# A token list made by one-hot products and gathered expert tiles in place of scattered ones, in a deformable convolution with a mixture-of-experts FFN

## The chip, the cores and the metric

One core of a Trainium2 chip runs the whole program. The metric is the device time of one execution, in microseconds; the kernel before has a median of 8195.0 us over nine runs (8178.31 to 8216.84). Everything is in float32.

## The reference

The input x is 4 images of 256 channels, 64 by 64. The layer computes

```python
x = x + conv3(ln_c(x))            # three deformable 3x3 convolutions, each with relu
t = to_tokens(x)                  # 4 images of 4096 tokens of 256 values
t = t + ffn(ln_t(t))
```

A deformable convolution computes 27 offset channels with an ordinary 3x3 convolution: a shift (dy, dx) and a mask for each of the 9 taps and each pixel. For each tap it samples the input bilinearly at the shifted place, multiplies by the mask, and multiplies the 256 sampled channels by that tap's 256x256 weights; the nine products are summed.

The FFN has 8 experts. A softmax over 8 gate logits picks the two likeliest experts of a token, and

```python
for e in range(8):
    h = gelu(xf @ w1[e] + b1[e])          # 256 -> 512
    out += cw[:, e:e+1] * (h @ w2[e] + b2[e])   # 512 -> 256
```

where cw is the softmax value at the two chosen experts and 0 elsewhere. So each token needs only two of the eight, and the kernel computes only these.

## The kernel before

**Convolution.** There are 12 stages, one for each image and layer. A stage has 8 blocks of 512 pixels, and a block 9 taps, so the program has 864 taps in all (`main_block`, L437 to L505). For each tap, POOL issues four indirect DMAs g (L452), each of which fetches for 128 pixels a row of 4 KB from a table in DRAM that holds two neighbouring pixels, values and differences. DVE interpolates in one direction (L458), ACT scales the first neighbour (L463), DVE adds the second (L468), PE transposes the samples (L472), ACT copies them out of PSUM (L477), and PE multiplies them with the tap's weights into `acc` (L480). The g buffers number ten, so POOL can run about two and a half taps ahead. The offset convolutions, the tables of the next layer and the gate of finished images are cut into pieces that `step` inserts after taps.

**The FFN, one group an image.** A group has M = 32 token tiles of 128 and NF = 39 expert tiles of FT = 256 slots (two chosen experts a token make 8192 slots, or 32 tiles, and each of the 8 experts may leave a tile partly filled). `tokens` writes t (the residual) and z (the normalised tokens) to DRAM and computes gate weights. When an image's last block is done, `enqueue` (L820) puts the group's steps in a queue, each with a price in taps:

- `route` (price 0) counts how many tokens go to each expert and gives each of a token's two choices a slot number; the slots of one expert begin at a multiple of 256. It also makes `wrow`, the rows of the weight table for every expert tile. Where a tile has the same expert as the tile two before, which used the same buffer, the rows are put out of bounds, and the fetch moves nothing.
- `dispatch_load` and `dispatch`: z is loaded again in blocks of 4 tiles (`zl`, L675, on SP), and each of the 64 pieces of 128 tokens is scattered by POOL to its slots in a DRAM array `zs` (L681). A dispatch step is one token tile with two scatters and costs 0.5 taps.
- 39 `expert` steps: POOL fetches the weights of the next tile (`w`, L706, 128 rows of 9.2 KB, two buffers), SP loads 256 slots of z (`zt`, L726), PE transposes them (`ftp`, L739), multiplies with W1 (`ph`, L750), ACT applies gelu (`hT`, L760), PE multiplies with W2 (`py`, L765), DVE adds the bias (`y`, L773), and SP stores y to `ys`.
- 16 `combine` steps: each of two token tiles; t is loaded in blocks of four tiles (`ta`, L783, on SP), POOL gathers each token's two results (`gy`, L794), DVE adds them with their weights (L802), PE transposes, and SP stores the output (L816).

`pump` (L837) runs after every tap and takes steps from the queue as the credit of one per tap allows. Groups 0 and 1 are spread over 2.9 stages each (the expert tiles 4.25 taps apart), group 2 over 1.9 (2.40 taps apart). Group 3 belongs to the last stage; its steps run after all convolution, with nothing beside them, and are called the tail here.

Each engine runs its instructions in one order, which a scheduler fixes when the program is built from the order of the calls and its own estimates; an instruction that waits holds up all behind it on its engine or queue. On POOL these are g, the scatters, w and gy, all indirect DMAs. Every buffer's reuse is a wait: the second w buffer is free when `y` of the tile that used it has read its bias.

`ffn_constants` writes zeros to the two `zs` arrays at the start (38 DMAs of 512 KB and 2 of 256 KB on SP), so that empty slots hold finite numbers.

Of the kernel before, what the change touches and what calls it, by code (L numbers as in the profile page):

```python
# [8 lines left out]
F32 = mybir.dt.float32  # L9
I32 = mybir.dt.int32  # L10
AF = mybir.ActivationFunctionType
ALU = mybir.AluOpType
AX = mybir.AxisListType
WAIT, ORDER = (
    mybir.DependencyInfo(c, mybir.DependencyReason.DATA)
    for c in (mybir.DependencyClass.Sync, mybir.DependencyClass.NoSync)
)

P = 128
H = W = 64  # L20
C = 256
CC = C // P
K = 9
NL = 3
TPB = 4
BLK = P * TPB
NB = H * W // BLK
# [8 lines left out]
E = 8  # L36
# [3 lines left out]
FT = 1 << FT_LOG  # L40
FU = FT // P
# [31 lines left out]
class Group:  # L73


    def __init__(self, b, n0, n1):
        self.b, self.n0, self.n1 = b, n0, n1
        self.nm = f"{b}_{n0}"
        self.M = (n1 - n0) * TPB

        self.NF = 2 * self.M * P // FT + E - 1
        self.scatters = []


class Weave:
# [83 lines left out]
    def ffn_constants(self):  # L169
        nc, cst, ins = self.nc, self.cst, self.ins  # L170
        self.t_dram, self.z_dram = (
            [
                [
                    self.dram.tile([P, TPB, C], F32, name=f"{v}_{b}_{n}", tag=f"{v}_{b}_{n}")
                    for n in range(NB)
                ]
                for b in range(self.B)
            ]
            for v in ("t", "z")
        )  # L180
        nf = max(g.NF for g in self.groups)
        self.zs, self.ys = (
            [
                self.dram.tile([nf * FT, C], F32, name=f"{v}_{i}", tag=f"{v}_{i}")
                for i in range(2)
            ]
            for v in ("zs", "ys")
        )

        nil = self.big.tile([P, 4 * C], F32, tag="a", name="nil")  # L190
        nc.vector.memset(nil, 0.0)
        for z in self.zs:
            r = 0
            while r < nf * FT:
                k = min(4 * P, nf * FT - r)
                nc.sync.dma_start(
                    z[r : r + k, :].rearrange("(p q) c -> p (q c)", p=P), nil[:, : k // P * C]
                )
                r += k
        self.gw = cst.tile([P, CC, E], F32, name="gw")  # L200
# [26 lines left out]
        nc.vector.tensor_copy(self.part, part_i)  # L227
        tile_i = cst.tile([P, nf], I32, name="tile_i")
        nc.gpsimd.iota(tile_i, pattern=[[1, nf]], base=0, channel_multiplier=0)
        self.tile_f = cst.tile([P, nf], F32, name="tile_f")  # L230
        nc.vector.tensor_copy(self.tile_f, tile_i)

# [278 lines left out]
    def tokens(self, b, n, r):  # L511
# [4 lines left out]
        if n == grp.n0:  # L516
            grp.cw = self.rt2.tile([P, 2, grp.M], F32, tag="cw", name=f"cw_{grp.nm}")
            grp.sel = self.rt.tile([P, 2, E, grp.M], F32, tag="sel", name=f"sel_{grp.nm}")
            grp.slots = self.rt2.tile([P, 2, grp.M], I32, tag="slots", name=f"slots_{grp.nm}")
            grp.wrow = self.rt2.tile([P, grp.NF], I32, tag="wrow", name=f"wrow_{grp.nm}")  # L520
        xc = self.big.tile([P, CC, BLK], F32, tag="a", name=f"xr_{nm}")
# [17 lines left out]
        normalise(nc, self.small, tok, z, self.eps_t, nm)  # L539
        nc.sync.dma_start(self.z_dram[b][n], z)  # L540
        for t0 in range(0, TPB, 2):
# [68 lines left out]
    def route(self, grp):  # L610
# [36 lines left out]
        for i in range(2):  # L647
# [8 lines left out]
            past,  # L656
            self.tile_f[:, :NF].unsqueeze(2).to_broadcast([P, NF, E]),
            end.unsqueeze(1).to_broadcast([P, NF, E]),
# [8 lines left out]
        same = small("same", (P, NF))  # L667
        nc.vector.memset(same[:, 0:2], 0.0)
        nc.vector.tensor_tensor(same[:, 2:], ex[:, 2:], ex[:, : NF - 2], ALU.is_equal)
        nc.vector.scalar_tensor_tensor(rows, same, float(E * P), rows, ALU.mult, ALU.add)  # L670
        nc.vector.tensor_copy(grp.wrow, rows)

    def dispatch_load(self, grp, n):
        z = self.ffn.tile([P, TPB, C], F32, tag="c", name=f"zl_{grp.nm}_{n}")
        self.nc.sync.dma_start(z, self.z_dram[grp.b][grp.n0 + n])  # L675
        grp.z = z

    def dispatch(self, grp, n, t):
        m = n * TPB + t
        for i in range(2):  # L680
            ins = self.nc.gpsimd.indirect_dma_start(  # L681
                out=self.zs[grp.i % 2],
                out_offset=bass.IndirectOffsetOnAxis(ap=grp.slots[:, i, m : m + 1], axis=0),
                in_=grp.z[:, t, :],
                in_offset=None,
            ).ins


            if len(grp.scatters) > 1:
                self.tc.add_manual_dep(ins, grp.scatters[0].name, ORDER)  # L690
            if grp.scatters:
                self.tc.declare_no_dep(
                    ins, group=f"zs_{grp.nm}", keep=grp.scatters[:1] if len(grp.scatters) == 1 else (), reason="slots differ"
                )
            self.tc.add_to_no_dep_group(f"zs_{grp.nm}", ins)
            grp.scatters.append(ins)

    def weights(self, grp, f):
        if self.w is None:
            self.w = [  # L700
                self.wt.tile([P, 2, WINN], F32, tag="wt", name=f"w_{i}").rearrange(
                    "p a b -> p (a b)"
                )
                for i in range(2)
            ]
        self.nc.gpsimd.indirect_dma_start(  # L706
            out=self.w[f % 2][:, : W1N + W2N],
            out_offset=None,
            in_=self.ins["W"],
            in_offset=bass.IndirectOffsetOnAxis(ap=grp.wrow[:, f : f + 1], axis=0),  # L710
            bounds_check=E * P - 1,
            oob_is_err=False,
        )

    def expert(self, grp, f):

        nc = self.nc
        nm = f"{grp.nm}_{f}"
        if f == 0:
            self.weights(grp, 0)  # L720
        if f + 1 < grp.NF:
            self.weights(grp, f + 1)
        w = self.w[f % 2]
        w1, w2 = w[:, :W1N], w[:, W1N : W1N + W2N]
        zt = self.ffn.tile([P, FU, C], F32, tag="zt", name=f"zt_{nm}")
        load = nc.sync.dma_start(  # L726
            zt,
            self.zs[grp.i % 2][f * FT : (f + 1) * FT, :].rearrange("(p u) c -> p u c", u=FU),
        ).ins
        if f == 0:  # L730
            for s in grp.scatters[:-1]:
                self.tc.add_manual_dep(load, s.name, WAIT)
            grp.load = load
        else:
            self.tc.add_manual_dep(load, grp.load.name, ORDER)
        tp = self.ps.tile([P, CC, FT], F32, tag="tp", name=f"ftp_{nm}")
        for u in range(FU):
            for c in range(CC):
                nc.tensor.transpose(  # L739
                    tp[:, c, u * P : (u + 1) * P], zt[:, u, c * P : (c + 1) * P], self.ident  # L740
                )
# [21 lines left out]
        for u in range(FU):  # L763
# [12 lines left out]
        nc.sync.dma_start(  # L776
            self.ys[grp.i % 2][f * FT : (f + 1) * FT, :].rearrange("(p u) c -> p u c", u=FU),
            y,
        )

    def combine_load(self, grp, n):
        a = self.ffn.tile([P, TPB, C], F32, tag="c", name=f"ta_{grp.nm}_{n}")
        self.nc.sync.dma_start(a, self.t_dram[grp.b][grp.n0 + n])  # L783
        grp.acc = a

    def combine(self, grp, n, t0):
        nc = self.nc
        nm = f"{grp.nm}_{n}_{t0}"
        acc = grp.acc
        for t in range(t0, t0 + 2):  # L790
            m = n * TPB + t
            for i in range(2):
# [13 lines left out]
        for t in range(2):  # L806
            for c in range(CC):
                nc.tensor.transpose(
                    tp[:, c, t * P : (t + 1) * P],
                    acc[:, t0 + t, c * P : (c + 1) * P],  # L810
                    self.ident,
                )
# [7 lines left out]
    def enqueue(self, grp):  # L820

        nb = grp.n1 - grp.n0
        q = [(0, lambda: self.route(grp))]
        for n in range(nb):
            q.append((3 if n == 0 else 0, lambda n=n: self.dispatch_load(grp, n)))
            for t in range(TPB):
                q.append((0.5, lambda n=n, t=t: self.dispatch(grp, n, t)))
        taps = grp.stages * NB * K - (3 + 2 * nb + 4 + 4 + 2 * nb)
        for f in range(grp.NF):
            q.append((taps / grp.NF if f else 4, lambda f=f: self.expert(grp, f)))  # L830
        for n in range(nb):
            q.append((0 if n else 4, lambda n=n: self.combine_load(grp, n)))
            for t0 in range(0, TPB, 2):
                q.append((1, lambda n=n, t0=t0: self.combine(grp, n, t0)))
        self.queue += q
# [102 lines left out]
```

## Time and profile before

The profiled execution took 8198.5 us, 3.5 above the median; its span, from the first to the last instruction, is 8196.6 us.

| engine | busy us | share |
|---|---|---|
| PE (matmul) | 6740.6 | 82% |
| PEld (weight load, beside PE) | 3773.7 | 46% |
| DVE | 4918.2 | 60% |
| ACT | 3568.6 | 44% |
| POOL | 4506.9 | 55% |

| stage (us) | what runs beside the convolution |
|---|---|
| 2472 to 2663, 4412 to 4600, 6236 to 6442 | scatters of groups 0, 1, 2 |
| 2700 to 3700, 4700 to 5600 | experts of groups 0, 1 |
| 6478 to 7382 | experts of group 2 |
| 7390 to 7590 | combine of group 2, last blocks of convolution |
| 7666 to 8197 | tail: scatters, experts and combine of group 3, no convolution |

DMA moved 2314.45 MB, of which queue 0, that of all indirect DMAs, moved 1954.99 MB. The TensorE clock that was granted averages 0.922 of full speed.

A profile line such as `L681 POOL DMA_INDIRECT zs<-zl,slots x256 | 265.2, 1036 | 137.8 <-issue 71.9` reads: line 681, engine, operation, output and inputs, 256 of them; 265.2 us busy in all, 1036 ns each; the engine was idle 137.8 us just before them, and 71.9 us of it ended for no other reason than that the instruction was issued. A line of waits reads: who waited, for which instruction, how many us in all, how often, and the longest. An indirect DMA on POOL is busy while its descriptors are made; the data come later.

### The profile page before, as it was taken

How to read it: one execution, taken by the hardware profiler on the slowest of the kernel's cores; microseconds unless marked ns; L12 is line 12 of the kernel's file. 1: busy time of each engine (PE TensorE's matmuls, PEld its weight loads, DVE VectorE, ACT ScalarE, POOL GpSimd, SP SyncE). 2: the span in 40 equal slices, each digit the busy share in tenths (PEclk: the TensorE clock that was granted, in tenths of full speed). 3: DMA queues.
4: the chain of work that ended last, by engine and by line, in shares of the span. 5: the costliest groups of instructions: out<-in, count | busy, mean ns of one | idle time of the engine just before them, and what ended most of it. 6: DMA issues, size and time to landing. Idle time of an engine off the chain costs nothing. (4 is left out here: it accounts for less than half of the span.)

```text
span 8196.6 us, 91172 instructions
## 1 busy us (share of the span) xinstructions
PE 6740.6 (82%) x27032; PEld 3773.7 (46%) x27032; DVE 4918.2 (60%) x10768; ACT 3568.6 (44%) x7368; POOL 4506.9 (55%) x4133
## 2 busy tenths in 40 slices
PE   5898888888886999998867799999856889896395
PEld 2344334344442555555433455555532455563274
DVE  4776666667774666666665566667755555665201
ACT  3454444445542444545443444545433344443121
POOL 0564666566556566664566666665666554546413
PEclk8999999999998999999987999999978899998697
DMA  5987889889887898998787889998877777777433
GB/s 167 364 312 276 311 302 323 298 315 332 294 307 247 310 328 312 324 324 296 258 290 254 277 313 338 321 333 312 295 274 260 253 286 261 291 282 267 145 124 118
DMA packets 744472, 2314.45 MB, mean 282 GB/s; under 512 B 104345, under 2 KB 148377, under 8 KB 735785
## 3 DMA queue, kind: packets, MB, share of 16 engines
q0 software_dynamic: 544704, 1954.99, 67.5%
q1 hardware_dynamic: 199272, 353.64, 12.3%
q8 instruction: 216, 3.54, 0.2%
q14 instruction: 280, 2.29, 0.1%
HBM read 2167.35 MB, written 249.61 MB: 295 GB/s over the span
## 5 line engine op out<-in xcount | busy, mean ns | idle before, releaser
L452 POOL DMA_INDIRECT g<-tab,idx x3456 | 3800.6, 1100 | 2681.2 <-DVE s L468 1317.9
L480 PE MATMUL acc<-sT,wk 128*128 128x512 f32 x6912 | 3443.1, 643 | 383.0 <-ACT sT L477 249.7
L458 DVE SCALAR_TENSOR_TENSOR g<-g,cf 128x512 f32<-128x512 f32 x3456 | 2529.3, 745 | 451.8 <-DMA g<-tab,idx 358.1
L468 DVE SCALAR_TENSOR_TENSOR s<-g,cf,s 128x256 f32<-128x256 f32 x3456 | 1619.0, 482 | 1610.1 <-ACT s L463 1208.8
L463 ACT ACTIVATE s<-g,cf 128x256 f32<-128x256 f32 x3456 | 1674.1, 511 | 1669.4 <-DVE g L458 1127.7
L480 PEld LDWEIGHTS acc<-sT,wk 128*128 128x128 f32 x6912 | 1344.8, 204 | 2093.8 <-issue 1548.3
L472 PE MATMUL tp<-ident,s 128*128 128x128 f32 x6912 | 1085.4, 284 | 455.5 <-DVE s L468 313.1
L477 ACT COPY sT<-tp 128x512 f32<-128x512 f32 x1728 | 970.9, 587 | 1103.2 <-PE tp L472 685.2
L472 PEld LDWEIGHTS tp<-ident,s 128*128 128x128 f32 x6912 | 828.2, 145 | 939.7 <-issue 514.0
L765 PE MATMUL py<-w,hT 128*128 128x256 f32 x2496 | 636.1, 391 | 65.7 <-ACT hT L760 58.6
L750 PE MATMUL ph<-fzT,w 128*128 128x256 f32 x2496 | 619.2, 391 | 25.0 <-ACT fzT L743 11.9
L750 PEld LDWEIGHTS ph<-fzT,w 128*128 128x128 f32 x2496 | 479.7, 195 | 171.3 <-issue 49.1
L765 PEld LDWEIGHTS py<-w,hT 128*128 128x128 f32 x2496 | 458.2, 192 | 205.4 <-ACT hT L760 119.3
L706 POOL DMA_INDIRECT w<-in_W,wrow x156 | 178.3, 1143 | 647.8 <-issue 291.5
L760 ACT ACTIVATE hT<-ph,w 128x256 f32<-128x256 f32 x624 | 261.3, 470 | 522.6 <-PE ph L750 343.6
L328 PE MATMUL po<-win,wo 128*32 128x512 f32 x2304 | 451.8, 612 | 36.7 <-ACT win L263 24.8
L773 DVE TENSOR_TENSOR y<-py,w 128x512 f32<-128x512 f32 x156 | 107.6, 690 | 464.2 <-PE py L765 455.7
L794 POOL DMA_INDIRECT gy<-ys,slots x256 | 261.6, 1022 | 212.4 <-DVE ta L802 92.9
L681 POOL DMA_INDIRECT zs<-zl,slots x256 | 265.2, 1036 | 137.8 <-issue 71.9
L298 ACT COPY hv<-tpv 128x512 f32<-128x512 f32 x384 | 214.6, 595 | 194.6 <-PE tpv L293 133.7
L328 PE MATMUL po<-win_pre,wo 128*32 128x512 f32 x1152 | 231.8, 654 | 23.9 <-ACT win_pre L263 7.4
L739 PE MATMUL ftp<-ident,zt 128*128 128x128 f32 x624 | 99.6, 282 | 96.1 <-DMA zt<-zs 93.9
(144 smaller groups left out, 3305.1 us busy)
## 6 DMA issues: line engine op xcount, KB each, us to landing
tab<-hv SPq DMA_DIRECT2D x384, 256.0 KB
g<-tab,idx POOLq DMA_INDIRECT x3456
zt<-zs SPq DMA_DIRECT2D x156, 256.0 KB
ys<-y SPq DMA_DIRECT2D x156, 256.0 KB
wk<-in_conv_w SPq DMA_DIRECT2D x108, 256.0 KB
zs<-nil SPq DMA_DIRECT2D x38, 512.0 KB
xc_pre<-in_x SPq DMA_DIRECT2D x32, 512.0 KB
xr_tok<-in_x SPq DMA_DIRECT2D x32, 512.0 KB
```

Source lines behind the costliest of these rows:

```text
L328: nc.tensor.matmul(po[g * Q : (g + 1) * Q, :], lhsT=self.wo[l][:, k, c, :], rhs=w[:, c, ky : ky + RPB, kx : kx + W], start=(m < NQ), stop= ...
L452: nc.gpsimd.indirect_dma_start(out=g.rearrange("p x s f -> p (x s f)"), out_offset=None, in_=tb, in_offset=bass.IndirectOffsetOnAxis(ap=id ...
L458: nc.vector.scalar_tensor_tensor(g[:, :, 0, :], g[:, :, 1, :], cf[:, j, 0:1], g[:, :, 0, :], ALU.mult, ALU.add,)
L463: nc.scalar.activation(s, g[:, 0, 0, :], AF.Copy, scale=cf[:, j, 1:2])
L468: nc.vector.scalar_tensor_tensor(ss[u], gs[u][:, 1, 0, :], cf[:, j, 2:3], ss[u], ALU.mult, ALU.add)
L472: nc.tensor.transpose(tp[:, c, u * P : (u + 1) * P], ss[u][:, c * P : (c + 1) * P], self.ident,)
L477: nc.scalar.copy(sT[:, :, t0 * P : (t0 + 2) * P], tp)
L480: nc.tensor.matmul(acc[:, o, :], lhsT=self.wk[k][:, c, o * P : (o + 1) * P], rhs=sT[:, c, :], start=(k == 0 and c == 0), stop=(k == K - 1 ...
L681: ins = self.nc.gpsimd.indirect_dma_start(out=self.zs[grp.i % 2], out_offset=bass.IndirectOffsetOnAxis(ap=grp.slots[:, i, m : m + 1], axis=0),
L750: nc.tensor.matmul(ph[:, h, :], lhsT=w1[:, o : o + P], rhs=zT[:, c, :], start=(c == 0), stop=(c == CC - 1),)
L765: nc.tensor.matmul(py[:, u, :], lhsT=hT[h // 2][:, h % 2, u * P : (u + 1) * P], rhs=w2[:, h * C : (h + 1) * C], start=(h == 0), stop=(h == ...
L794: nc.gpsimd.indirect_dma_start(out=g, out_offset=None, in_=self.ys[grp.i % 2], in_offset=bass.IndirectOffsetOnAxis(ap=grp.slots[:, i, m : ...
```

## The change

The scatter of tokens to slots is replaced by its inverse. After `route`, every group makes a list `tok` that holds for each slot the number of the token in it, and the expert tiles gather their tokens by it.

- z is stored row by row in one DRAM array per group (`zd`). The arrays `zs`, their zero fill, the loads `zl` and the scatters are gone.
- `route` splits each slot number into slot & 127 and slot >> 7. An `invert` step, one token tile at a price of 0.25 taps, does the following twice (once for each choice): DVE compares a row of 0 to 127 with the low digit (`at`, 128x128), compares a row of 0 to 77 with the high digit and multiplies with the token number (`num`, 128x78), and PE adds at-transposed times num into a PSUM tile `inv` (128x78). After the 32nd step the sums are copied to `tok`, integers: column j of row p is the token in slot 128 j + p. Empty slots hold 0, so token 0 is computed there and never read.
- `fetch` issues on POOL, one step ahead of an expert tile, the weights w and two gathers zt of 128 rows of 1 KB by columns of `tok`, in two buffers for each half.
- The tiles are taken in the order 0, 20, 1, 21, 2, ...: even steps walk through the first half of the list and odd steps through the second, and each half has its own weight buffer. A fetch moves nothing when the tile before it in the list has the same expert.
- y is stored with the two halves of a tile one after the other in `ys`, which fits the order of `tok`.
- t is loaded for each pair of token tiles (256 KB in place of 512), and the load of the next pair is put ahead of the combine step of this one.
- Prices: inversion takes 8 taps in place of the dispatch's 16 and the rest is shared by the expert tiles, 4.46 taps apart in groups 0 and 1 and 2.61 in group 2.

```diff
+        self.half = (self.NF + 1) // 2
+        self.zt, self.acc = {}, []
+        self.order = [s // 2 + s % 2 * self.half for s in range(self.NF)]
...
-        for z in self.zs:
-            r = 0
-            while r < nf * FT:
-                k = min(4 * P, nf * FT - r)
-                nc.sync.dma_start(
-                    z[r : r + k, :].rearrange("(p q) c -> p (q c)", p=P), nil[:, : k // P * C]
-                )
-                r += k
+        for g in self.groups:
+            g.zd = self.dram.tile([g.M * P, C], F32, name=f"z_{g.nm}", tag=f"z_{g.nm}")
...
-        nc.vector.memset(same[:, 0:2], 0.0)
-        nc.vector.tensor_tensor(same[:, 2:], ex[:, 2:], ex[:, : NF - 2], ALU.is_equal)
+        nc.vector.tensor_tensor(same[:, 1:], ex[:, 1:], ex[:, : NF - 1], ALU.is_equal)
+        nc.vector.memset(same[:, 0 : grp.half + 1 : grp.half], 0.0)
...
-    def dispatch(self, grp, n, t):
-        m = n * TPB + t
+    def invert(self, grp, m):
+        nc = self.nc
+        lo, hi = grp.digits
+        n = FU * grp.NF
         for i in range(2):
-            ins = self.nc.gpsimd.indirect_dma_start(
-                out=self.zs[grp.i % 2],
-                out_offset=bass.IndirectOffsetOnAxis(ap=grp.slots[:, i, m : m + 1], axis=0),
-                in_=grp.z[:, t, :],
-                in_offset=None,
-            ).ins
...
+            at = self.ffn.tile([P, P], F32, tag="at", name=f"at_{nm}")
+            nc.vector.tensor_scalar(at, self.row_f, lo[:, i, m : m + 1], None, ALU.is_equal)
+            num = self.ffn.tile([P, n], F32, tag="num", name=f"num_{nm}")
+            nc.vector.tensor_scalar(
+                num, self.row_f[:, :n], hi[:, i, m : m + 1], self.token[:, m : m + 1],
+                ALU.is_equal, ALU.mult,
+            )
+            nc.tensor.matmul(
+                grp.inv, lhsT=at, rhs=num,
+                start=(m == 0 and i == 0), stop=(m == grp.M - 1 and i == 1),
+            )
+        if m == grp.M - 1:
+            nc.vector.tensor_copy(grp.tok, grp.inv)
...
-    def expert(self, grp, f):
+        grp.zt[step] = []
+        for u in range(FU):
+            zt = self.ffn.tile([P, C], F32, tag=f"zt{u}", name=f"zt_{grp.nm}_{f}_{u}")
+            j = FU * f + u
+            self.nc.gpsimd.indirect_dma_start(
+                out=zt,
+                out_offset=None,
+                in_=grp.zd,
+                in_offset=bass.IndirectOffsetOnAxis(ap=grp.tok[:, j : j + 1], axis=0),
+            )
+            grp.zt[step].append(zt)
+
+    def expert(self, grp, step):
...
-        load = nc.sync.dma_start(
-            zt,
-            self.zs[grp.i % 2][f * FT : (f + 1) * FT, :].rearrange("(p u) c -> p u c", u=FU),
-        ).ins
...
-        for n in range(nb):
-            q.append((3 if n == 0 else 0, lambda n=n: self.dispatch_load(grp, n)))
-            for t in range(TPB):
-                q.append((0.5, lambda n=n, t=t: self.dispatch(grp, n, t)))
-        taps = grp.stages * NB * K - (3 + 2 * nb + 4 + 4 + 2 * nb)
+        for m in range(grp.M):
+            q.append((0.25 if m else 3, lambda m=m: self.invert(grp, m)))
+        taps = grp.stages * NB * K - (3 + nb + 4 + 4 + 2 * nb)
```

In the changed kernel the product of the inversion is L692, w L709, the gathers of tokens L721, ftp L744, y L778, g L442 and the s update of DVE L458.

## The prediction

> **What bounds the kernel now.** I read the page first (engine shares, then the groups of POOL and the expert phase). No engine is full over the whole span, so the limits have to be found by stage. The rows that the change touches:
>
> ```profile
> PE 6740.6 (82%) x27032; PEld 3773.7 (46%) x27032; DVE 4918.2 (60%) x10768; ACT 3568.6 (44%) x7368; POOL 4506.9 (55%) x4133
> ...
> L706 POOL DMA_INDIRECT w<-in_W,wrow x156 | 178.3, 1143 | 647.8 <-issue 291.5
> ...
> L681 POOL DMA_INDIRECT zs<-zl,slots x256 | 265.2, 1036 | 137.8 <-issue 71.9
> ...
> L739 PE MATMUL ftp<-ident,zt 128*128 128x128 f32 x624 | 99.6, 282 | 96.1 <-DMA zt<-zs 93.9
> ```
>
> PE is 82% busy, the scatters L681 hold POOL 265 us, and one wait of 93.9 us stands ahead of a transpose of zt.
>
> Second, the busy times by stage (columns: us, then PE, PEld, DVE, ACT, POOL busy, clock, DMA share, GB/s):
>
> ```profile
> 2472.00:2663.00 191.00, 121.03 (x430) 56.65 (x430) 80.13 (x179) 56.87 (x117) 124.99 (x118) 0.81 0.75 255
> 2700.00:3700.00 1000.00, 956.21 (x3996) 550.68 (x3989) 663.85 (x1360) 498.12 (x1055) 616.08 (x544) 0.99 0.90 321
> 4412.00:4600.00 188.00, 127.92 (x447) 58.96 (x445) 80.97 (x178) 58.09 (x121) 120.00 (x114) 0.79 0.73 248
> 6236.00:6442.00 206.00, 122.55 (x354) 54.13 (x353) 79.62 (x150) 54.79 (x110) 138.84 (x132) 0.78 0.73 250
> 6500.00:7340.00 840.00, 752.34 (x3123) 486.79 (x3122) 478.90 (x990) 367.16 (x788) 407.24 (x385) 0.96 0.76 276
> 7666.00:7754.00 88.00, 0.00 (x0) 0.00 (x0) 1.03 (x5) 0.00 (x0) 64.36 (x66) 0.50 0.50 168
> ```
>
> Experts of groups 0 and 1 beside convolution (2700 to 3700) are bound by PE: 96% busy, clock 0.99. The three stretches in which slots are scattered have PE at 59 to 68% and DMA at 0.73 to 0.75: no unit is full, so something is in series. The last scatter, with no convolution beside it, leaves PE idle for 88 us.
>
> Third, convolution taps per stage, counted by DVE's s updates (L468, four a tap):
>
> ```profile
> 2700.00:3700.00 1000.00, 243.69 (x517) 0.99 0.90 321
> ...
> 2472.00:2663.00 191.00, 28.55 (x61) 0.81 0.75 255
> 4412.00:4600.00 188.00, 29.28 (x62) 0.79 0.73 248
> 6236.00:6442.00 206.00, 30.60 (x64) 0.78 0.73 250
> ```
>
> A tap takes 1000/(517/4) = 7.74 us beside experts, but 12.5, 12.1 and 12.9 us beside scatters. POOL explains it: an indirect DMA starts 1.27 us after the one before (0.97 busy + 0.30), and four table gathers and four scatters a tap are 10.2 us. That is the series.
>
> Fourth, POOL's waits in the experts of group 2, which come every 23.8 us (39 y between 6478 and 7382) where groups 0 and 1 need 33 to 35, and one of these waits in order of time:
>
> ```profile
> POOL w L706 <- issue: 202.8, 26, 20.4
> POOL g L452 <- issue: 81.2, 258, 2.0
> ```
>
> ```profile
> 6659.17 1.14 POOL L452 DMA_INDIRECT g<-tab,idx  x1 [0.30 <-issue]
> 6672.69 1.41 POOL L706 DMA_INDIRECT w<-in_W,wrow  x1 [12.38 <-issue]
> 6674.41 0.94 POOL L452 DMA_INDIRECT g<-tab,idx  x1 [0.30 <-issue]
> ```
>
> The weight fetch w waits until y of two tiles before has left DVE (y began at 6671.22), and every g of the taps to come is queued behind it: 12.38 us without a gather, after which they follow at 1.25 us. So POOL's order, not its load, is the weak place of group 2.
>
> **The change part by part** (against the profiled execution, 8198.5 us, of which the span is 8196.6; it is 3.5 above the median of 8195.0).
>
> *Scatters of groups 0 to 2 go.* The three stretches hold 187/4 = 46.75 taps and take 585 us; at 7.74 a tap they would take 362: 223 us go. zl loads on SP (32) go with them.
>
> *Inversion comes.* Each group gets 32 steps, four a tap, so 8 taps. A step is two of: a 128x128 compare, a 128x78 compare-and-scale, one f32 product. No row has these shapes. On DVE, tensor-scalar rows bound them: 0.211 (128x72) to 0.416 (128x256); I take 0.28 and 0.22, hence 8 x 0.50 = 4.0 us a tap. Convolution beside experts keeps DVE 663.85/129.25 = 5.1 us a tap, so DVE alone allows 9.1. But at and num have two buffers each, and PE takes each pair in its own order between the taps' products, so DVE and PE wait for each other: I take 11.2 a tap, and 5 us a group until the list is copied out and the first tokens land. 24 x (11.2 - 7.74) + 15 = +98. The low end is DVE's 9.1 (+33); the high end is 15.7 a tap, which the first six taps beside group 2's scatters took by the same count (24 updates from 6236 to 6330; +206). PE's 16 records a tap at about 0.15 (138 records in 21.2 us, L739) are 2.4 us inside that. With the 223 above: -125 (-190 to -17).
>
> *Tail dispatch.* slots are ready at 7667, the first ftp starts at 7754.4: 87 us. In its place 64 pairs: DVE 0.50, PE two records at 0.15 (warm) to 0.30 (clock 0.50): 0.6 a pair is 38 us; the digits, the copy and a gather (gy rows land 2.7 to 3.4 us after issue) about 5. So -44; at 0.9 a pair, were PE and DVE to wait out each other, -24; at DVE's bare 0.42 a pair, -55.
>
> *Tokens are gathered on POOL, not loaded by SP.* 312 gathers at 1.27 = 396 us of POOL against 256 scatters (325) removed. In groups 0 and 1, 2.5 us more per 34 us: POOL waits there 237 us of 1000 for DVE (it is ahead of need), so I take 0 (0 to +40). If that cover were gone, each step would cost 2.5.
> In group 2 it meets the wait above. Read statically from the two instruction orders, w stood on average 1.5 taps behind the y that it waits for, in the second half of the group over 2; now it stands 1.0 behind throughout, because the inversion ends 8 taps earlier and a step has 2.61 taps for 2.40. Behind w come two token gathers ahead of the next g. The token gathers wait for ftp of two tiles before, 2 to 4 taps back: not late. POOL's loop per step: before 2.40 x 4 x 1.27 + 1.4 = 13.6 plus a mean wait of 202.8/26 = 7.8, 21.4 of the 23.8. After: 2.61 x 4 x 1.27 + 1.4 + 2.5 = 17.2 plus the wait. A step at today's 9.9 us a tap is 25.8; with a wait of 10.2, between 7.8 and 12.4, POOL's loop is 27.4: 38 x 1.6 = +60. Ends: 0 at the old mean wait, less 20 for weights that no longer come (below), and +145 if every w waits the 12.38 shown (29.6).
>
> The Trainium skill, "DMA: Bandwidth & Descriptors" (Issuing engine by pattern), speaks against this move: simple loads belong on Sync, only indirect ones on GPSIMD, and the former path is said to be generally faster. Its fit (Anatomy of one DMA) gives 2.0 + 131072/436e3 = 2.3 us for a 128 KB gather, an estimate; by it nothing would be lost, as the tokens have two taps or more to land. By the row it is not landing but the issue, 1.27 us in order on POOL, that costs.
>
> *Weights.* Queue 0 moved 1954.99 MB; table gathers are 3456 x 0.524 = 1811.9, scatters and gy 33.55 each; the rest is 64 fetches of 1.18 MB, 16 a group. With the halves a buffer keeps its expert over consecutive steps: 9 or 10 a group. Where PE is bound it is hidden. In the tail the 38 steps take 326.5 us, 13.2 more than at the steady 8.245: half goes, -6 (0 to -13).
>
> *Combine in the tail* loads one pair ahead in 256 KB: DVE waits 13.2 us for ta there; -8 (0 to -13). Beside convolution 0: it has taps of lead.
>
> *Zero fill* (20 MB at the start): from 200 to 300 us 48 gathers were issued where 57 are in the next 100; 9 x 1.75 = 16, of which the trend of the start may be a part: -12 (0 to -16). z is stored in rows of 1 KB, ys too: as many bytes on SP, off the path, 0.
>
> Sum: -125 - 44 + 60 - 6 - 8 - 12 = -135, so 8063; against the median, 8060.
>
> **The rivals.**
> 1. *POOL's queue takes it all: slower.* Place: w of group 2. Price: (17.2 + wait - 25.8) x 38. A mean wait of 15 gives +243 instead of +60: 8243. It decides from about 14.2 us on (+213, with which the sum is past 8195 + 16). For it: waits up to 20.4 today and the lead of one tap; against it: the mean of 7.8 and fewer weights behind w.
> 2. *The inversion is as dear as the scatter.* 15.7 us a tap and 0.9 a tail pair: -17 and -24 in place of -125 and -44: 8188, no change that can be told. For it: two buffers across two in-order engines, and idle PE loses clock (0.79 beside scatters). Against: half as many taps.
> 3. *More is won.* DVE's bare 9.1 a tap (-190), no loss in group 2, and 20 won from lighter queues: -190 - 44 - 20 - 26 = -280: about 7915. For it: about 100 MB of 2314 less to move (scatters 34, zl 17, zeros 20, weights 31). Against: nothing in the experts of groups 0 and 1 waits for DMA.
>
> On PE's clock, the Trainium skill, "TensorE: Matmul & The Clock Gate" (What's actually happening), halves it after an idle window of about 3.4 us and restores it after one of sustained work; the 0.50 while PE idled agrees. Were the products enough to keep it full, the pair would be DVE's 0.50 and the tail dispatch 6 us shorter still.
>
> **How the numbers follow.** Forecast 0.52, rival 1 0.18, rival 2 0.10, rival 3 0.20. The forecast's own spread is about 90 either way (the ends above, not all at once). The range 7910 to 8225 cuts the dearer half of rival 1 and the outer half of rival 3. About 0.2% (16 us) is what a measurement can tell from no change: faster 0.76 (all of 3, nearly all of the forecast, half of 2), same 0.08, slower 0.16 (most of 1).
>
> **What would show it.** Right: taps at about 11 us over 8 taps in place of 12.5 over 15.5 thrice, with L692 on PE; ftp some 43 us after slots in the tail; POOL's w (L709) waiting some 10 us a step in group 2, with DVE waiting for g behind it; queue 0 near 1955 - 34 + 41 - 31 = 1931 MB. Wrong: POOL's w or zt waiting in groups 0 and 1, where I cost them at nothing, inversion taps over 15 us, or group 2 steps over 30 us.

## The result, and the profile after

The changed kernel has a median of 8296.1 us (10 runs) against 8193.4 us for the kernel before, a ratio of 1.0125 with an interval of 1.0109 to 1.0141: it is slower by 103 us. The profiled execution has a span of 8286.7 us, 90.1 more than before. The forecast was 8060, and 8296 lies above its range.

That is not the whole result. The chips that ran these two kernels and the experiments are of two kinds, and the sign of the change depends on which. On chips of the first kind the kernel before takes 8076 to 8193 us; on those of the second kind it takes 7753 to 7760. On the second kind the changed kernel was measured twice, at 0.9788 (0.9772 to 0.9804) and 0.9784 (0.9765 to 0.9803): faster by 2.1%. All that follows names the kind.

The rows of the page of the changed kernel (first kind) that answer to those shown of before:

```profile
PE 6877.6 (83%) x27544; PEld 3866.5 (47%) x27544; DVE 5038.3 (61%) x11300; ACT 3566.4 (43%) x7359; POOL 4521.0 (55%) x4189
...
q0 software_dynamic: 547392, 1929.26, 67.4%
...
L709 POOL DMA_INDIRECT w<-in_W,wrow x156 | 174.5, 1118 | 572.6 <-issue 481.6
...
L721 POOL DMA_INDIRECT zt<-z,tok x312 | 334.1, 1071 | 158.4 <-issue 85.2
```

PE gained 137 us, about the 512 products of the inversion (0.275 us each in the median), DVE 120 and POOL 14: beside the inversion nothing was added that would fill 100 us. The busy times by stage (us, then PE, PEld, DVE, ACT, POOL, clock, DMA share, GB/s):

```profile
2421.00:2504.00 83.00, 80.07 (x394) 45.08 (x394) 72.57 (x234) 34.41 (x69) 38.08 (x34) 0.98 0.76 254
2700.00:3700.00 1000.00, 870.51 (x3457) 485.33 (x3455) 575.79 (x1163) 426.29 (x904) 555.93 (x521) 0.94 0.80 273
...
6600.00:7440.00 840.00, 716.29 (x2893) 452.57 (x2886) 441.33 (x915) 345.40 (x730) 438.52 (x413) 0.92 0.71 246
7780.00:7850.00 70.00, 45.93 (x154) 35.50 (x152) 45.70 (x173) 6.61 (x10) 2.00 (x2) 0.57 0.13 49
```

And the s updates of DVE in two of these, from which the taps are counted:

```profile
2421.00:2504.00 83.00, 14.94 (x33) 0.98 0.76 254
2700.00:3700.00 1000.00, 210.08 (x445) 0.94 0.80 273
```

Of POOL's waits in the experts of group 2 (6600 to 7440):

```profile
POOL w L709 <- issue: 198.5, 23, 14.0
POOL g L442 <- issue: 99.7, 278, 14.7
```

The wait at w is 8.6 us each where it was 7.8. The inversion, 2421 to 2504, has PE and DVE near full, and its eight taps take 83 us, 10.4 each. The loss is in the second row: beside the experts of group 0, PE fell from 96% busy to 87%, its clock from 0.99 to 0.94, and a tap takes 1000/(445/4) = 8.99 us in place of 7.74.

With the moment of each tap's last s update, the span splits into stages of equal work. Profiled executions, us; the last two columns are both of the second kind:

| stage | before, first kind | after, first kind | difference | difference, second kind |
|---|---|---|---|---|
| start to tap 295 | 2458.5 | 2420.6 | -38 | -27 |
| scatter or inversion and the taps up to the first expert, three groups (295 to 314, 511 to 530, 727 to 746) | 690.9 | 499.8 | -191 | -116 |
| experts of group 0 (324 to 468) | 1146.9 | 1296.6 | +150 | +4 |
| experts of group 1 (540 to 684) | 1114.7 | 1281.8 | +167 | +36 |
| experts of group 2 (746 to 838) | 893.7 | 963.7 | +70 | -9 |
| tail, after tap 863 | 564.0 | 507.4 | -57 | -50 |

The few taps between these stages make up the rest, -11 us on the first kind and -4 on the second.

### The profile page after: what moved, and what is told of

Same layout as the page of the kernel before. It is cut to its first block, busy times and chain, and to the rows that moved or that the text cites. A ratio compares the mean times of both kernels' runs of the same rounds, so it can differ in the third digit from the quotient of the medians.

```text
span 8286.7 us, 92385 instructions
## 1 busy us (share of the span) xinstructions
PE 6877.6 (83%) x27544; PEld 3866.5 (47%) x27544; DVE 5038.3 (61%) x11300; ACT 3566.4 (43%) x7359; POOL 4521.0 (55%) x4189
## 3 DMA queue, kind: packets, MB, share of 16 engines
q0 software_dynamic: 547392, 1929.26, 67.4%
## 5 line engine op out<-in xcount | busy, mean ns | idle before, releaser
L442 POOL DMA_INDIRECT g<-tab,idx x3456 | 3743.6, 1083 | 2812.5 <-DVE s L458 1482.2
L458 DVE SCALAR_TENSOR_TENSOR s<-g,cf,s 128x256 f32<-128x256 f32 x3456 | 1617.7, 481 | 1679.9 <-ACT s L453 1294.6
L709 POOL DMA_INDIRECT w<-in_W,wrow x156 | 174.5, 1118 | 572.6 <-issue 481.6
L721 POOL DMA_INDIRECT zt<-z,tok x312 | 334.1, 1071 | 158.4 <-issue 85.2
L778 DVE TENSOR_TENSOR y<-py,w 128x512 f32<-128x512 f32 x156 | 107.7, 691 | 362.9 <-PE py L770 327.5
L283 PE MATMUL tpv<-ident,vv 128*128 128x128 f32 x768 | 157.1, 285 | 16.1 <-ACT sT L467 15.6
```

The source lines that it names most:

```text
L442: nc.gpsimd.indirect_dma_start(out=g.rearrange("p x s f -> p (x s f)"), out_offset=None, in_=tb, in_offset=bass.IndirectOffsetOnAxis(ap=id ...
L458: nc.vector.scalar_tensor_tensor(ss[u], gs[u][:, 1, 0, :], cf[:, j, 2:3], ss[u], ALU.mult, ALU.add)
L721: self.nc.gpsimd.indirect_dma_start(out=zt, out_offset=None, in_=grp.zd, in_offset=bass.IndirectOffsetOnAxis(ap=grp.tok[:, j : j + 1], axi ...
```

## The experiments

Three theories of the loss in groups 0 and 1 (317 us on the first kind). **O**: the two token gathers, where they stand, lead the scheduler to another order on PE. As the built program has it, a tap's product follows its own last transposes with less than 0.6 us of other PE work between (counted by the profile's pitches) in 42% and 44% of the taps of the two groups, against 15% and 16% before; I call these taps without cover. **S**: tiles 4.46 taps apart fall on the same taps of every block of nine. In the changed kernel y lands on two of the nine taps in nearly every block, and PE idles ahead of the product of taps 3 and 8. **G**: the gathers delay by their own work.

The first four runs fell on another chip of the first kind, where the kernel before takes 8090 us. Neither that kernel nor the changed one was profiled there, so the stages of the four runs are set against the profiles above, from where it takes 8193; the ratios are against the kernel before on their own chip.

**Tokens by SP loads.** The gathers go, all else stays; the experts compute on the wrong tokens.

```diff
-            self.nc.gpsimd.indirect_dma_start(out=zt, ..., in_=grp.zd, in_offset=... grp.tok[:, j : j + 1] ...)
+            r0 = j * P % (grp.M * P)
+            self.nc.sync.dma_start(zt, grp.zd[r0 : r0 + P, :])
```

> The changed kernel with one thing different: the tokens of an expert tile are loaded by SP as 128 plain rows of zd in order, in place of POOL's gather by the list (so the experts compute on the wrong tokens; the list is still made). Spacing of the tiles, inversion, weights, combine stay. Theory O (order): the two gathers a tile make the scheduler lay PE's order differently. In the changed kernel a tap's product stands directly behind its own last transposes in 42 to 44% of the taps beside the experts of groups 0 and 1, against 15 to 16% before; PE then waits for ACT's copy, its clock falls, and this is the whole 150 us lost in each of the two groups. With SP loads the share is 16 to 19% again, so groups 0 and 1 return to 7.8 to 8.0 us a tap, the granted clock there to 0.99, and the time falls by 250 to 350, to about 7980. Theory S (spacing): tiles 4.46 taps apart fall on the same two taps of every block of nine; the spacing is unchanged, so groups 0 and 1 stay at 8.8 to 9.0 us a tap; only group 2 gains its POOL waits, to about 8220. Theory G (the gathers themselves delay tokens or table rows on POOL and in DMA): like O in the time, but then DVE or PE waits for g or zt in the changed kernel, of which the traces show almost nothing.

First kind: ratio 0.9616 (0.9593 to 0.9639). Its groups 0 and 1 in the busy times by stage:

```profile
2615.00:3763.00 1148.00, 1085.85 (x4524) 624.65 (x4523) 774.62 (x1620) 574.83 (x1209) 672.58 (x611) 0.99 0.88 311
4438.00:5559.00 1121.00, 1061.29 (x4403) 615.38 (x4402) 753.90 (x1555) 562.45 (x1180) 675.63 (x611) 1.00 0.89 316
```

The whole 317 us are gone (+1 and +6 against the profile of before) with the spacing at 4.46, and the clock is back at 0.99 and 1.00. By the ratios some 410 us came back, more than O's 250 to 350, as group 2 fell too, to 876 us (before 894, the change 964). So the gathers are the cause, by O or by G, and S by itself costs nothing.

**Spacing of before.**

```diff
-        taps = grp.stages * NB * K - (3 + nb + 4 + 4 + 2 * nb)
+        taps = grp.stages * NB * K - (3 + 2 * nb + 4 + 4 + 2 * nb)
```

> The changed kernel with the expert tiles as far apart as before (4.25 and 2.40 taps in place of 4.46 and 2.61, the eight taps given back at the end of a group). Theory S: groups 0 and 1 recover their 300 us, to about 7990. Theory O: the share of taps whose product stands directly behind its own transposes falls only from 42 to 44% to 33 to 35%, so a third of the loss returns at most: 8190 to 8290. Theory G: the gathers are the same, no recovery, 8280 or more.

First kind: 0.9991 (0.9973 to 1.0009). Groups 0 and 1 took 1231 and 1209 us: 65 and 72 of the 150 and 167 came back, nearer to O's third than to S's all, and rather more than O had said.

**The kernel before with gathers**, from the scattered array with a fixed list of rows.

```diff
-        load = nc.sync.dma_start(zt, self.zs[...][f * FT : (f + 1) * FT, :]...)
+        for u in range(FU):
+            load = nc.gpsimd.indirect_dma_start(
+                out=zt[:, u, :], in_=self.zs[grp.i % 2], in_offset=... self.rowno[:, FU * f + u : FU * f + u + 1] ...)
```

> The kernel before with one thing different: the 256 rows of an expert tile are fetched from the scattered array by two POOL gathers with a fixed list of rows (the same rows, the same result) in place of one SP load. Scatters, spacing 4.25 and weights stay as before. Theory O: the share of taps without cover rises from 15 to 16% to 28 to 31%, so about half of the changed kernel's loss appears in groups 0 and 1: 60 to 100 us each, and some in group 2, about 8350. Theory S: the spacing is that of before, groups 0 and 1 keep 7.8 to 8.0 us a tap: 8195 to 8250. Theory G: the full loss of 150 a group, 8450 to 8550.

First kind: 1.0352 (1.0324 to 1.0380). The total fits G's figure, not O's. By stage it is mixed: groups 0 and 1 take 1211 and 1194 us, 64 and 79 over the profile of before, as O had it; group 2 takes 977, 84 over, which O left vague. The gathers alone, in the kernel before, cost more than the whole change.

**Forced order.** A product is bound behind the first half of the next tap's transposes, and nothing else changes.

```diff
+                if t0 == 0 and held is not None:
+                    product(*held, after=last)     # the product of tap k, ordered behind these transposes of tap k + 1
```

> The changed kernel with all its gathers, spacing and work, and one more ordering rule: PE's product of a tap is issued after the first half of the next tap's transposes (within a block). Theory O: taps without cover fall to 4%, so groups 0 and 1 return to about 7.8 to 8.0 us a tap with a clock of 0.98 or more and the time falls by 250 to 350, to about 7980; where DMA is the limit (stages without experts) it makes no difference or a loss of some 0.1 us a tap. Theory S: the tiles still fall on the same taps, little changes, 8250 to 8300. Theory G: POOL and the DMA do the same work in the same order, so no change, 8250 to 8300.

First kind: 0.9908 (0.9880 to 0.9937). Groups 0 and 1:

```profile
2631.00:3815.00 1184.00, 1083.18 (x4516) 627.90 (x4515) 781.62 (x1623) 577.89 (x1209) 736.69 (x675) 0.98 0.86 301
4526.00:5688.00 1162.00, 1071.92 (x4394) 620.22 (x4393) 758.87 (x1554) 565.03 (x1183) 739.33 (x676) 0.98 0.87 304
```

The same gathers (x675 on POOL against x611 without them) in another order: 113 and 120 us of the 150 and 167 came back, and the clock with them, though a tap took 8.2 and 8.1 us and not 7.8 to 8.0. O holds for about three quarters of the loss in groups 0 and 1 (not quite two thirds, should all the 103 us by which the kernel before is faster on this chip lie there); 37 and 47 us stay with the gathers themselves. In the total O holds for less: the gain, 178 us by the ratios, is below the 250 expected and less than half of what the SP loads brought, as group 2 moved only from 964 to 948.

**The kernel before, forced** (the same edit in the other kernel).

> The kernel before with the ordering rule of the forced order alone (a tap's product issued after the first half of the next tap's transposes). Theory O: beside the experts of groups 0 and 1 the order was good already (15 to 16% of the taps without cover, now 1%), so these stages gain 0 to 20 us each; the 115 and 120 us that the same rule gave the changed kernel there are what its own order had cost. Rival (the rule is a general gain that has nothing to do with the gathers): these stages gain 80 us or more here too. Total: 8150 to 8200 by O on a chip where the kernel before takes 8193, 8000 by the rival.

Second kind: 0.9996 (0.9986 to 1.0007). The rule gives nothing to the kernel before. As it turned out, this chip says little of O: see below.

**SP loads, forced.**

> The changed kernel with tokens loaded by SP in plain rows (wrong tokens, as in the first run) and the ordering rule. It has neither the gathers nor the order that they brought. Theory O: groups 0 and 1 as in the SP load run, 1120 to 1150 us for 144 taps (ratio to before 0.955 to 0.965); what the forced order run takes above it there (37 and 47 us) is the gathers' own price on POOL and in DMA, and in group 2 (taps 746 to 838) about 70 us. Rival: it gains another 80 us or more a group over the SP load run, so order and gathers are independent gains.

Second kind: 0.9695 (0.9676 to 0.9715), groups 0 and 1 at 1127 and 1102 us, the first in O's range and the second below it; the ratio missed its range by little.

**Late fetch.** The weights and the gathers of the next tile become a step of their own, half a spacing after the expert step.

```diff
-        if step + 1 < grp.NF:
-            self.fetch(grp, step + 1)
...
-            q.append((taps / grp.NF if f else 4, lambda f=f: self.expert(grp, f)))
+            q.append((taps / grp.NF / 2 if f else 0, lambda f=f: self.expert(grp, f)))
+            if f + 1 < grp.NF:
+                q.append((taps / grp.NF / 2, lambda f=f: self.fetch(grp, f + 1)))
```

> The changed kernel with the fetch of the next tile (weights and the two gathers) issued as a step of its own, half a tile's spacing after the expert step, in place of at its beginning. Theory of the POOL queue: in group 2, w then stands 2.3 taps behind the y that it waits for in place of 1.0, POOL's waits at w (232 us) fall below 100, and taps 746 to 838 take 60 to 90 us less than the 964 of the changed kernel. In groups 0 and 1 the share of taps without cover falls from 42 to 44% to 21 to 26%, so by theory O they recover 80 to 100 us each: the ratio to before goes from 1.0125 to about 0.983. By a theory in which the gathers' work itself is the price, groups 0 and 1 stay at 1280 to 1300 us.

Second kind: 0.9757 (0.9739 to 0.9775), groups 0 and 1 at 1139 and 1115, group 2 at 801, POOL's waits at w there 116 us and not below 100. It looked like a full recovery, better than expected. That could not be told, as the changed kernel had not yet been measured on a chip of this kind.

**Late fetch, forced.**

> The changed kernel with both: the ordering rule and the late fetch. It does all that the changed kernel does. By O and the POOL queue together: groups 0 and 1 about 1160 us, taps 746 to 838 about 880 to 900: the ratio to before 0.982. If the late fetch only pushes the tokens behind more table gathers, group 2 stays at 948 and the ratio at 0.991.

Second kind: 0.9735 (0.9718 to 0.9753), better than expected and the lowest ratio of the kernels that compute everything.

**Before and after again, side by side, and the late fetch in its two halves.** Here the kind of chip came out.

> The kernel before, unchanged, for its profile on the same chip as the three runs beside it, since stages limited by DMA differ between chips. Groups 0 and 1 (PE limited) 1080 to 1150 us for 144 taps, clock 0.99.

> The changed kernel, unchanged, on the same chip. Ratio to before 1.008 to 1.018; groups 0 and 1 150 us over the kernel before, group 2 (taps 746 to 838) 70 us over it.

Second kind: before 7757.5 (7760.5 in the profiled execution), after 7594.6, ratio 0.9788. The expectation for the changed kernel was wrong in every number. The program is the same one, so its order is too: 42% and 44% of the taps without cover. But groups 0 and 1 take 1132 and 1125 us, with the clock at 1.00:

```profile
2569.00:3702.00 1133.00, 1071.56 (x4506) 617.07 (x4505) 777.49 (x1618) 576.24 (x1209) 732.56 (x675) 1.00 0.89 315
4366.00:5491.00 1125.00, 1058.26 (x4393) 611.09 (x4392) 759.44 (x1554) 564.63 (x1182) 737.97 (x675) 1.00 0.89 314
```

So the order alone is not the price either. What it meets on the first kind is seen in the waits between 4700 and 5600 us (who, for what, us in all, times, longest), first kind:

```profile
ACT sT L467 <- remote: 69.2, 20, 6.7
DVE s L458 <- issue: 64.2, 56, 6.0
PE acc L470 <- ACT sT L467: 62.7, 27, 6.1
```

and second kind, the same program (in the kernel before, on the first kind, this last wait comes to 11.2 us, 16 times, 1.5 at most):

```profile
PE acc L470 <- ACT sT L467: 26.9, 50, 0.9
```

"remote" marks a wait whose end the profile cannot explain. On the first kind ACT's copy of the transposes waits so 104 times in the changed kernel, 334 us in all, and 73 times, 293 us, in the kernel before; on the second kind no such wait exists in either. One of them in order of time, first kind:

```profile
5330.47 0.44 PE L462 MATMUL tp<-ident,s 128*128 128x128 f32 x2
5330.84 1.05 PE L318 MATMUL po<-win,wo 128*32 128x512 f32 x2
...
5337.21 0.58 ACT L467 COPY sT<-tp 128x512 f32<-128x512 f32 x1 [4.78 <-remote]
5337.85 5.69 PE L470 MATMUL acc<-sT,wk 128*128 128x512 f32 x8 [5.97 <-ACT sT L467]
```

and the same tap on the second kind:

```profile
4946.52 0.44 PE L462 MATMUL tp<-ident,s 128*128 128x128 f32 x2
4946.89 1.05 PE L318 MATMUL po<-win,wo 128*32 128x512 f32 x2
4947.00 0.59 ACT L467 COPY sT<-tp 128x512 f32<-128x512 f32 x1 [0.33 <-PE tp L462]
4947.86 3.70 PE L470 MATMUL acc<-sT,wk 128*128 128x512 f32 x8
```

By the profile, ACT's copy begins 6.3 us after the end of the transposes that it waits for on the first chip, and 0.04 us after on the second. PE has nothing but this tap's product ahead, so it idles 5.97 us, and the product itself then takes 5.69 us in place of 3.70 at a lower clock. In the trace of the semaphores PE's results come more than 1 us after the modelled end 369 times in the changed kernel and 293 times in the kernel before on the first kind, and twice on the second; those of DVE and ACT are never late more than twice. What holds PE up, the trace does not show. The traces of the first kind also lack about a fifth of these events (in the kernel before 3893 of PE's 4808 are there, and 8154 of DVE's 10177), those of the second kind next to none, so the counts are of what was recorded, and that the recording has a part in the delays is not excluded.

The Trainium skill, "TensorE: Matmul & The Clock Gate" (What's actually happening), halves the clock after an idle window of about 3.4 us. The two kinds agree with that: in groups 0 and 1 the changed kernel has 300 us at half clock on the first, where PE idles longer than 3.4 us 33 times (6.6 at most), and 3 us on the second, where it never does.

> The changed kernel with the weights fetched where they were, at the beginning of the expert step, and only the two token gathers issued half a spacing later. Share of taps without cover in groups 0 and 1: 26 to 28% (changed kernel 42 to 44%, late fetch 21 to 26%). Theory O: groups 0 and 1 recover 90 to 150 of their 150 us each. Theory of the POOL queue for group 2: w still stands one tap behind the y that it waits for, so POOL's waits at w stay above 150 us and group 2 stays 40 us or more over the kernel before; only the 2.5 us of the gathers behind w are gone.

> The changed kernel with the token gathers at the beginning of the expert step, and only the weights fetched half a spacing later. Share of taps without cover in groups 0 and 1: 18 to 23%. Theory O: groups 0 and 1 recover 110 to 150 of their 150 us each. Theory of the POOL queue for group 2: w stands more than two taps behind the y that it waits for, POOL's waits at w fall below those of the changed kernel by half, and group 2 comes within 20 us of the kernel before.

Second kind, where there was nothing to recover: 0.9800 (0.9784 to 0.9817) and 0.9804 (0.9787 to 0.9820), no better than the changed kernel beside them. They test O no more, but they do test POOL's queue: its waits at w in group 2 are 123.9 us in the changed kernel and

```profile
POOL w L709 <- issue: 62.3, 26, 12.0
```

with the weights late, half as expected, and 112.2 with the tokens late, where more than 150 was expected. Group 2 takes 820 us in the changed kernel (814 in a second profile), 804 with the weights late and 814 with the tokens late, and 828 in the kernel before. So the queue's place is real, and halving its wait is worth 10 to 15 us there, which the total does not show.

**Late fetch on the first kind.** Only there can it tell O from its rival. The next two comparisons fell on the second kind:

> The changed kernel, unchanged, beside the late fetch. If the kernel before takes about 8100 or more here: ratio 1.008 to 1.018, groups 0 and 1 at 1250 to 1300 us for 144 taps, with waits that end for nothing that the profile shows. If it takes about 7757: ratio 0.977 to 0.981, groups 0 and 1 at 1120 to 1135.

> The late fetch. Theory O (a tap's product without other work ahead of it turns every late result into idle PE): where the kernel before takes 8100 or more, the share of taps without cover is 21 to 26% in place of 42 to 44%, so groups 0 and 1 recover half to all of their 150 us each, and the ratio to before is 0.965 to 0.985. A rival (the late results come as often and cost as much, whatever the order): groups 0 and 1 stay above 1250 and the ratio above 1.0. Where the kernel before takes 7757: ratio 0.974 to 0.978, as before.

> The late fetch once more. Where the kernel before takes 8090 or more: by theory O ratio 0.965 to 0.985, groups 0 and 1 at 1130 to 1210 us for 144 taps; by the rival (late results cost the same whatever the order) above 1.0 and above 1250. Where it takes about 7757: 0.974 to 0.978, as twice before.

Second kind: the changed kernel 0.9784, the late fetch 0.9753 (0.9729 to 0.9777) and 0.9757 (0.9740 to 0.9773): all as expected there. The last one fell on the first kind:

> The late fetch once more, with the same two theories. Where the kernel before takes 8090 or more: by theory O ratio 0.965 to 0.985, groups 0 and 1 at 1130 to 1210 us for 144 taps; by the rival above 1.0 and above 1250. Where it takes about 7757: 0.974 to 0.978.

First kind (before 8075.6): 0.9853 (0.9825 to 0.9880). Groups 0 and 1:

```profile
2636.00:3834.00 1198.00, 1087.66 (x4494) 628.21 (x4492) 769.85 (x1616) 570.34 (x1205) 737.32 (x672) 0.98 0.85 296
4540.00:5716.00 1176.00, 1070.66 (x4365) 620.54 (x4363) 750.99 (x1551) 557.70 (x1176) 730.63 (x673) 0.97 0.86 298
```

98 and 107 us of the 150 and 167 come back with all gathers in place, and 60 of the 70 in group 2 (903.5 us): in O's range by the groups, a hair above its upper edge by the ratio, and far from the rival's. Together, on the first kind (late results: PE's events more than 1 us after the modelled end, in groups 0 and 1):

| kernel | taps without cover, groups 0 and 1 | late results | us over before, groups 0 and 1 |
|---|---|---|---|
| before | 15%, 16% | 37 | 0, 0 |
| tokens by SP | 16%, 19% | 34 | +1, +6 |
| forced order | 4%, 4% | 41 | +37, +47 |
| late fetch | 21%, 26% | 100 | +51, +60 |
| before with gathers | 28%, 31% | 82 | +64, +79 |
| spacing of before | 33%, 35% | 99 | +84, +95 |
| the change | 42%, 44% | 127 | +150, +167 |

With gathers the price rises with the share of taps without cover; about 40 us a group stay where there are next to none. The late results grow with it roughly, so order and gathers change not only what a late result costs but how often one comes; how the 317 us divide between the two, and why more come, is not shown. The rival as stated (as often and as dear, whatever the order) is ruled out: the late fetch has 100 of them for a third of the price. The profiles come from three chips of the first kind (before 8193 for the first and last rows, 8076 for the late fetch, 8090 for the others), so a few tens of us between rows are not to be leaned on. The four rows of one chip alone give the same picture: +7, +84, +143 and +179 us for the two groups. The late fetch beats both kernels on both kinds of chip: 0.9853 and 0.975 to 0.976.

## Why the prediction was wrong

- **The failed step is "In groups 0 and 1 ... so I take 0 (0 to +40)".** Measured: +317 for the two on the first kind, and +40, the end of the range, on the second. Its cover was real: POOL waited for w some 5 us between 4700 and 5600 and for DVE 285, so it was ahead of need, and the sign of being wrong that was named, POOL's w or zt waiting there, hardly came (zt 14 us in the same window). What the runs showed in its place is the order on PE: with the same gathers in a forced order, 233 of the 317 came back. I asked what the gathers do to POOL and to the tokens, and not what they do to the order of everything else. I had both orders, and used them for the distance of w, zt and ftp from what they wait for; the order of the taps themselves, transposes against product, I did not compare, and there the change had moved 27% of the taps in these groups from covered to without cover.
- **The second half of the failure was in the profile of before.** Waits that end for "remote" stood in its scatter stage (34.2 us for sT between 2472 and 2663), and I read past them. They are PE's late results; in groups 0 and 1 the kernel before recorded 37 of them and the change 127. On chips without them the forecast's ratio, 8060/8195 = 0.9835, compares with 0.9784 and 0.9788: right in sign, and short by 0.5%, in part by luck, as the +60 of group 2 did not come there (-9) and +40 came in groups 0 and 1.
- **Scatters and inversion, -125:** -191 on the first kind, -116 on the second. The inversion took 10.4, 10.1 and 9.4 us a tap, not 11.2, though num cost 0.33 and at 0.30 in place of 0.22 and 0.28: DVE and PE waited for each other less (DVE 7.0 us for inv in the 83 us of group 0). POOL's series of 10.2 us a tap, read as the whole price of the scatters, falls short of their 12.1 to 12.9; on the second kind the same scatter stages of the kernel before take 602 us in place of 691, so something besides POOL's series was in it, late results perhaps.
- **Tail, -44 -6 -8 = -58:** -57. Slots to first ftp 47.5 us in place of 87.4 (-40; a pair took 42.4/64 = 0.66, forecast 0.6); the y steps 313.6 in place of 326.5 (-13, the top of its bounds); combine -4.
- **Group 2, +60:** +70 on the first kind, but not shown to be for the reason given. POOL's waits at w were 8.6 us each, below the 10.2 taken. On the second kind the same queue costs nothing against before (-9), and there halving the wait gave 10 to 15 us. On the first kind forced order gave 16 of the 70 back and the late fetch, which moves w and the order both, 60. How the 70 divide between POOL and PE's late results is open.
- **Start, -12:** -38 on the first kind, -27 on the second: more than the one window showed. No run put the zeros back, so their share is not shown.
- **Weights:** queue 0 moved 1929.26 MB where 1931 was forecast.
- **Rivals.** The result is slower, as in rival 1, but not by its mechanism: 317 of the loss lie where POOL hardly waited for w. Rival 2 fell (9.4 to 10.4 us a tap). Rival 3 asked for 0.966; the best whole kernel reached 0.9735, on the second kind.
- The rule weighed there from the Trainium skill, "DMA: Bandwidth & Descriptors" (Issuing engine by pattern), that simple loads belong on Sync, held on the first kind by far: 0.9616 with SP loads against 1.0125, on two chips. On the second kind it is worth 0.4% (0.9695 against 0.9735, both in forced order, the latter with the late fetch). In groups 0 and 1 most of the price was the order; what the rest is, landing or POOL's issue, no run here tells apart.

## What to carry to other kernels

A DMA moved to another queue changes, through the scheduler, the order of instructions that have nothing to do with it; compare that order on the engine that binds, stage by stage, before costing the move at nothing. A product placed directly behind its own transposes cost little where every result was punctual (+4 and +36 us in groups 0 and 1 with all else of the change) and some 115 us a stage where some came late, so work between producer and consumer is worth having even where a trace shows no wait. And a few per cent measured on one chip may have the other sign on the next: run both kernels side by side on more than one.

## What the runs showed of the hardware

- Two kinds of chip: the same program, the kernel before, takes 8076 to 8193 us on one and 7753 to 7760 on the other. The engines' own durations are the same (the s update 482 and 480 ns, the copy of transposes 587 and 587 ns, the transposes 284 and 284 ns). The difference is in waits that nothing in the profile ends: "remote" 557 us and none, "issue" 5178 and 3269 us by the list of waits. As the traces of the first kind lack a fifth of the engines' semaphore events, part of the second difference may be in the telling of waits and not in the waits.
- On the first kind PE's results come up to several us late (293 events more than 1 us late in the kernel before, 369 in the changed kernel); DVE's and ACT's do not. The cause was not found.
